# Pooling: a row's coefficients made among its elder neighbour's chunks and held, its outputs transposed into the places of u and v

## The chip, the cores and the metric

The kernel runs on one core of a Trainium2 chip. The metric is the device time of one execution in microseconds (us), the median of three runs. Five engines share the core's on-chip memory: TensorE (PE in the profile, its weight loads PEld), VectorE (DVE), ScalarE (ACT), GpSimd (POOL) and SyncE (SP), which only issues transfers here. Each engine works through its own instructions in a fixed order, and waits at the head of that order for what an instruction needs.

## The reference

The input x is 16 rows of 512 x 512 floats (512 positions S, 512 features D). Two residual blocks follow each other, both per row:

```python
h = gelu(x @ fc1_w.T + fc1_b)                                  # 512 -> 2048
x = x + concat([h @ fc2_w.T + fc2_b,                           # 384 features
                h @ experts_w[idx].T + experts_b[idx]], -1)    # 128 features, the row's expert
scores = tanh(x @ W1 + b1) @ v                                 # one number per position
mask = (l <= j, l >= j, l != j)[ptype]                         # one of three kinds per row
p = softmax(where(mask, scores, -1e30), -1)
x = x + (p @ x) / cnt                                          # the pooling
```

The three masks make the pooling of a row a running sum from the left, one from the right, or the sum of everything but the position itself. So no 512 x 512 product is needed: a recurrence along the positions, with coefficients made of the 512 scores, gives the result.

## The kernel before

The rows go in eight pairs i = 0..7. For a pair, fc1 is one Strassen-like product of 7 outer products, `Outer` n = 0..6, each of 7 inner products in two halves. An outer product is a loop of 14 steps k (a step is 4 matmul records in the trace, about 0.865 us of TensorE); the second half runs 5 steps behind the first, so that the last steps of an `Outer` run within the next one. After each inner product a short addition or copy brings its result from PSUM (the matmuls' output memory) to the on-chip memory: VectorE at L604, L618, L629, L641 and L645, ScalarE at L602, L620 and L625, with gelu at L591, GpSimd at L632. PSUM has few banks (three "bx", three "by", one "bd"), so TensorE's later product waits for these. GpSimd also makes the differences of the next outer product's input (`outer_sum` L292, `inner_sums` L314). Then come fc2 of row 0 and fc2 of row 1 (products "1", "2", "5", "7", "6", "3", "4"), whose result is x1T, the row after the first block, transposed.

The pooling of a finished row is a `Pooling` object, worked off a little at a time beside later matmuls. `project` and `score` (L851, L860) make the scores on TensorE; ScalarE copies them to two short rows `srow` (L863, L864), and two DMAs bring them into s2, a 32 x 16 layout (L867). What follows is a Python generator, `run_all`:

- `weights` (L969 to L1071): 43 small VectorE instructions, most on 32 x 16 numbers, and one exp on ScalarE (L1018), turn scores to coefficients. MAX8 and FIND_INDEX8 (L982, L984) find the largest score, and `at_maximum` lets GpSimd read x at its position (L934). The coefficients go to a DRAM tile `co_d` by two DMAs and come back as `cb`, spread over all 128 partitions (L1086 then mirrors a part).
- `apply`, for each of four chunks dc of 128 features: `weigh` (u = x1T times a coefficient, L1114, L1117), `recur` (the scan along the positions, L1125, and U, L1126), `offset` (ScalarE makes v, L1151, L1152), `finish` (f and the addition into x1T, L1133, L1143). u and v have one buffer each of 128 x 1024, f two of 128 x 512.
- four `flip`s: VectorE transposes x1T's chunk back by 32 x 32 blocks into a tile `yo` (L1193), and four DMAs store it to the output. The tag "yo" has two buffers, which `srow` and the last row's `spread` use as well.

The generator yields an estimate of its VectorE time after each bit, or a negative number for a pause. The order is written out by hand: `slot(SPARE[n], 0.86)` after each step of fc1, `slot(SPARE_2[name], 3.4)` within fc2. `Pooling.slot` takes bits from the generator until the slot's budget is used up. The function `slot` serves only the oldest unfinished row in the list `pools`; the next row's steps begin when it is done. `drain(1)` after fc1 and `drain()` after row 0 run what is left at once. SP's queue issues the weight loads (a ring of ten tiles of 256 KB), and co_d, cb and the output stores; ScalarE's queue issues s2 and the residual's input.

The even row of a pair has its coefficients in fc2 of row 1, its `apply` at the end of row 1 and in n = 0..2 of the next pair's fc1, with the flips in n = 4 and 5. The odd row is projected at k = 6 and scored at k = 11 of n = 0 of that fc1; its coefficients come at n = 5, n = 6 and in row 0, its `apply` and flips at the end of row 0. The last two rows, 14 and 15, have their own arrangement at the end.

Of the kernel before, what the change touches and what calls it, by code (L numbers as in the profile page):

```python
# [9 lines left out]
F32 = mybir.dt.float32  # L10
# [7 lines left out]
def tile_cond_experts_then_prompt_pool(  # L18
# [17 lines left out]
    P = 128  # L36
    B, _, ND, S = xT.shape
# [21 lines left out]
    p1 = ctx.enter_context(tc.tile_pool(name="p1", bufs=1))  # L59
# [104 lines left out]
    class Ring:  # L164
        def __init__(self):
            self.plan, self.tiles = [], {}
            for i in range(B // 2):
                b = 2 * i
                for o in OUTER:
                    self.plan += [("f1", i, o, p) for p in (INNER if i else INNER_0)]  # L170
                for r in range(2):
                    self.plan += [("up", b + r, "a11", h) for h in range(4)]
                    if not r:
                        self.plan += [("ex", b, "a11", h) for h in range(2)]
                    self.plan += [("up", b + r, "a12", h) for h in range(4)]
                    self.plan += [("ex", b + r, "a12", h) for h in range(2)]
                    self.plan += [("lo", b + r, n, h) for n in LOWER for h in range(2)]
                    if not r:
                        self.plan += [("ex", b + 1, "a11", h) for h in range(2)]
            self.at = 0  # L180
            self.taken, self.free = [], set()
# [135 lines left out]
    def bank(tag, name):  # L317
        return ps_m.tile([P, 2, HC], F32, tag=tag, name=name, bufs={"bx": 3, "by": 3, "bd": 1}[tag])
# [510 lines left out]


    TAGS = ("bx", "bx", "bx", "bd")
    co_d = dram.tile([2, ROW], F32, name="co_d")

    class Pooling:


        def __init__(self, b, x1T):
            self.b, self.x1T = b, x1T
            self.last = b == B - 1
            self.queue = nc.gpsimd if b == B - 2 else nc.sync  # L840
            self.turn = nc.vector.snap(nc.vector.value_load(ptype[b : b + 1].unsqueeze(0), min_val=0, max_val=2) % 2)
            self.steps = self.run_all()
            self.pause = self.credit = 0
            self.sent = False
            self.done = False

# [22 lines left out]
        def last_scores(self):  # L869

            self.y = [bank(t, f"y_{k}").rearrange("p m s -> p (m s)") for k, t in enumerate(TAGS)]
            for dc in range(ND):
# [22 lines left out]
            return copy  # L895


        def slot(self, budget, passed):
            self.pause -= passed
            if self.pause > 0:  # L900
                return
            self.credit = min(self.credit + budget, max(budget, 3.5))
            while self.credit > 0 and not self.done:
                t = next(self.steps, None)
                if t is None:
                    self.done = True
                elif t < 0:
                    if budget < 1e6:
                        self.pause = -1.7 * t
                        if passed < 1:  # L910
                            self.credit = 0
                        return
                else:
                    self.credit -= t
# [7 lines left out]
        def at_maximum(self, i8):  # L922
            b, eng = self.b, nc.scalar if self.last else nc.gpsimd
            jm = eng.value_load(i8[0:1, 0:1], min_val=0, max_val=S - 1)
            if self.last:
                jm = eng.snap((jm % SG) * SL + jm // SG)
                self.j_fix = jm
            self.x_max = self.x1T[:, :, ds(jm, 1)].rearrange("p k o -> p (k o)")
            self.xm = p1.tile([P, ND], F32, tag="xm", name=f"xm_{b}")
            self.eng = eng  # L930
            if self.last:
                eng.activation(self.xm, self.x_max, AF.Copy, scale=is2[:, b : b + 1])
            else:
                eng.tensor_tensor(self.xm, self.x_max, is2[:, b : b + 1].to_broadcast([P, ND]), ALU.mult)  # L934

        def run_all(self):
            yield from self.weights()
            yield from self.apply()
            if self.b < B - 3:
                yield -2  # L940
                for dc in range(ND):
                    store = self.flip(dc)
                    yield 0.7
                    yield -1
                    store()
                    yield -1

        def weights(self):
            V, b = nc.vector, self.b
            W = 32  # L950

            def small(name, shape, dt=F32):
                return p1.tile(shape, dt, tag=f"c_{name}", name=f"{name}_{b}")
# [99 lines left out]
            t = small("t", [SG, SL])  # L1053
# [23 lines left out]
            row = co_d[b % 2]  # L1077
            self.queue.dma_start(row[: 3 * S].rearrange("(k p c) -> p k c", k=3, c=SL), co)
            self.queue.dma_start(row[3 * S : 3 * S + 3].unsqueeze(0), sc[0:1, :3])
            yield -2  # L1080
            cb = self.cb = p1.tile([P, ROW + 2 * S], F32, tag="cb", name=f"cb_{b}")
            self.sent = True
            self.queue.dma_start(cb[:, 2 * S : ROW + 2 * S - 1], row[: ROW - 1].partition_broadcast(P))
# [105 lines left out]

        def flip(self, dc, yo=None):  # L1190
            if yo is None:
                yo = p1.tile([P, S], F32, tag="yo", name=f"yo_{self.b}_{dc}", bufs=2)
            nc.vector.transpose(yo, self.x1T[:, dc, :])  # L1193
            to = out[self.b].rearrange("(c j) (k a i) -> k a j c i", j=32, a=4, i=32)

            def store():
                for a in range(4):
                    nc.sync.dma_start(to[dc, a], yo[ts(a, 32), :].rearrange("j (c i) -> j c i", i=32))

            return store  # L1200
# [7 lines left out]
    pools = []  # L1208

    def slot(budget, passed):  # L1210
        while pools and pools[0].done:
            pools.pop(0)
        if pools:
            pools[0].slot(budget, passed)

    def drain(left=0):
        while len(pools) > left:
            slot(1e9, 1e9)


# [10 lines left out]
    for i in range(B // 2):  # L1231
# [9 lines left out]
        for n in range(7):  # L1241
# [8 lines left out]
            for k in range(14):  # L1250
# [29 lines left out]
                if n or k >= 8:  # L1280
                    slot(SPARE[n], 0.86)
# [4 lines left out]
        if i == 0:  # L1286
# [3 lines left out]
            flush_stores()  # L1290
            xr_next[:] = [residual(0, 0, 0), residual(0, 1, 1)]
        drain(1)
        for row in range(2):
            b = b0 + row
# [3 lines left out]
            def at(name):  # L1298
# [40 lines left out]
                if b + 1 == B:  # L1339
                    if name == "1b":  # L1340
                        pool.rush()
                    elif name == "2":
                        before_last.flip_all("xT")
                    elif name == "end":
                        pool.flip_all("tx")
                    elif name in LAST_2:
                        slot(LAST_2[name], 1.7)
                elif row and name == "4a":

                    slot(SPARE_2["3m"] * 0.4, 5.1)  # L1350
                elif name in SPARE_2 and not (row and name in ("3m", "3", "4m")):
                    slot(SPARE_2[name] * (0.4 if row and name in ("7m", "6m") else 1), 3.4)
                if b + 1 == B and name == "3":
                    drain()

            psc, x1T = fc2(b, hT[:, row], experts, at)
            if row == 0:
                experts = nxt["ex"]
                drain()
            elif more:  # L1360
                x_next, xi_next, xi_after = nxt["x"], nxt["xi"], nxt["xi_2"]
# [47 lines left out]
```

## Time and profile before

| | before |
|---|---|
| median of 3 runs | 1599.04 us (1598.66 to 1599.4) |
| the profiled execution | 1603.34 us, of which the span on the core is 1601.6 us |
| mean granted TensorE clock | 0.992 of full speed |
| one pair's fc1 (pairs 1 to 7) | 90.5 to 92.4 us |
| one row's fc2 | 101.1 us |
| first pair's fc1, tail after the last fc2 | 99.9 us, about 25 us |
| input read, output written | 253.55 MB, 29.45 MB |

The profiled execution is one execution with a profiler beside it. Its busy times are per engine; since the engines work beside each other they don't add up to the span. A line of the timeline gives start, duration, engine, source line, operation, output and inputs by name, and in square brackets how long the engine stood idle before it and what ended that. A line of the waits gives who waited for whom, the time in total, how often, and the longest one.

### The profile page before, as it was taken

To read this page: it belongs to the slowest core of one execution; us is meant where nothing else is said; L and a number is where in the kernel's file an instruction comes from. 1 tells how busy PE (TensorE), PEld (TensorE's weight loads), DVE (VectorE), ACT (ScalarE), POOL (GpSimd) and SP (SyncE) were. 2 spreads that over 40 slices of the span, in tenths; PEclk is the share of its full clock that TensorE was granted. 3 is DMA by queue.
4 is the path that set the end of the run, shared out by engine and by line. 5 is a ranking of instruction groups with operands and counts; after the bars stand their busy time and mean duration, and the time that the engine had idled before them with its cause. 6 is when DMAs were issued, how large, how long until landed. Compare 5 with 4: busy or idle time off the path is not lost. (4 is left out here: it accounts for less than half of the span.)

```text
span 1601.6 us, 21969 instructions
## 1 busy us (share of the span) xinstructions
PE 1565.5 (98%) x6986; PEld 1317.3 (82%) x6986; DVE 1160.8 (72%) x2108; ACT 620.9 (39%) x1244; POOL 391.7 (24%) x426
## 2 busy tenths in 40 slices
PE   7999999999999999999999999999999999999996
PEld 6788878888788888888888887888878888788884
DVE  7874657957677676777678785786757867668776
ACT  2350145422453324633246223462244521454333
POOL 5641015200350004500054000630015200260020
PEclk9999999999999999999999999999999999999997
DMA  7666646658466574666656675566745658466442
GB/s 269 218 216 211 207 128 165 191 156 262 117 176 194 148 240 133 175 204 164 201 147 180 198 209 154 156 190 182 217 149 160 193 160 259 118 169 184 154 99 53
DMA packets 340094, 284.54 MB, mean 178 GB/s; under 512 B 145292, under 2 KB 264140, under 8 KB 339980
## 3 DMA queue, kind: packets, MB, share of 16 engines
q1 hardware_dynamic: 313580, 244.23, 53.4%
q0 software_dynamic: 5760, 19.97, 3.8%
q10 hardware_dynamic: 20640, 18.94, 3.7%
q8 instruction: 56, 0.92, 0.2%
q14 instruction: 58, 0.48, 0.1%
HBM read 253.55 MB, written 29.45 MB: 177 GB/s over the span
## 5 line engine op out<-in xcount | busy, mean ns | idle before, releaser
L591 ACT ACTIVATE hT<-hT,fc1b_sb 128x256 f32<-128x256 f32 x416 | 179.7, 498 | 65.0 <-DVE hT L645 50.7
L632 POOL TENSOR_TENSOR q<-p,hT 128x512 f32<-128x512 f32 x80 | 106.0, 1325 | 368.9 <-ACT p L625 365.1
L574 PE MATMUL bx<-xi,w_f_s_s 128*128 128x256 f32 x512 | 129.7, 385 | 5.0 <-DVE ba L618 2.6
L724 PE MATMUL ba<-hT,w_up_a 128*128 128x256 f32 x512 | 116.7, 381 | 0.0
L574 PEld LDWEIGHTS bx<-xi,w_f_s_s 128*128 128x128 f32 x512 | 96.2, 191 | 24.5 <-DVE ba L618 8.0
L724 PEld LDWEIGHTS ba<-hT,w_up_a 128*128 128x128 f32 x512 | 96.5, 190 | 23.1 <-issue 10.7
L724 PE MATMUL bb<-hT,w_up_a 128*128 128x256 f32 x512 | 113.1, 379 | 0.0
L724 PE MATMUL bd<-hT,e 128*128 128x256 f32 x496 | 112.1, 379 | 0.0
L724 PEld LDWEIGHTS bb<-hT,w_up_a 128*128 128x128 f32 x512 | 97.3, 190 | 13.2
L724 PEld LDWEIGHTS bd<-hT,e 128*128 128x128 f32 x496 | 94.2, 190 | 12.8
L464 POOL DMA_INDIRECT e<-in_expT,rows x32 | 33.0, 1031 | 278.9 <-PE bd L724 273.9
L604 DVE TENSOR_TENSOR hT<-bx,hT 128x512 f32<-128x512 f32 x112 | 75.4, 685 | 32.6 <-PE bx L574 32.3
L1086 ACT COPY cb<-cb 128x1024 f32<-128x1024 f32 x15 | 15.7, 1045 | 210.5 <-DMA cb<-co_d 181.7
L574 PE MATMUL bx<-xi,w_f_a_s 128*128 128x256 f32 x384 | 95.4, 381 | 1.2 <-ACT ba L620 0.5
L625 ACT COPY p<-bd 128x512 f32<-128x512 f32 x112 | 65.4, 584 | 74.8 <-PE bd L574 72.9
L629 DVE TENSOR_TENSOR by<-bx,p 128x512 f32<-128x512 f32 x112 | 77.6, 692 | 21.7 <-PE bx L574 21.2
L1151 ACT ACTIVATE v<-f,U,cb 128x512 f32<-128x512 f32 x60 | 48.9, 815 | 107.6 <-DVE U L1126 102.2
L1125 DVE TENSOR_TENSOR_SCAN f<-cb,u 128x512 f32<-128x512 f32 x60 | 79.6, 1327 | 12.9 <-ACT u L1117 12.3
L1193 DVE STREAM_TRANSPOSE yo<-x1T 128x512 f32<-128x512 f32 x60 | 41.2, 701 | 63.4 <-DMA out_y<-yo 61.0
L680 ACT ACTIVATE xr<-xr,fc2b_sb 128x256 f32<-128x256 f32 x96 | 44.9, 500 | 106.2 <-DVE p1x L743 50.9
L1133 DVE TENSOR_TENSOR f<-v,cb 128x512 f32 x60 | 46.1, 769 | 53.9 <-ACT v L1152 53.9
L574 PEld LDWEIGHTS bx<-xi,w_f_a_s 128*128 128x128 f32 x384 | 72.1, 190 | 13.3 <-ACT ba L620 2.1
(292 smaller groups left out, 3495.7 us busy)
## 6 DMA issues: line engine op xcount, KB each, us to landing
w_up_a<-in_fc2T SPq DMA_DIRECT2D x128, 256.0 KB
w_lo_s<-w2s_s SPq DMA_DIRECT2D x128, 256.0 KB
w_f_s_s<-w1s_s_s SPq DMA_DIRECT2D x112, 256.0 KB
w_f_a_s<-w1s_a_s SPq DMA_DIRECT2D x84, 256.0 KB
w_f_s_a<-w1s_s_a SPq DMA_DIRECT2D x84, 256.0 KB
w_f_a_a<-in_fc1T SPq DMA_DIRECT2D x69, 256.0 KB
w_ex_a<-in_fc2T SPq DMA_DIRECT2D x64, 256.0 KB
xr<-in_xT ACTq DMA_DIRECT2D x64, 256.0 KB
```

The source lines that it names most:

```text
L574: nc.tensor.matmul(to.rearrange("p (b s) -> p b s", b=2) if len(mv.shape) == 3 else to, w[:, ts(2 * mh + m, P)], mv, start=(not add and m ...
L591: nc.scalar.activation(to[:, m], src[:, m], AF.Gelu, bias=fc1b_sb[:, hc + m : hc + m + 1])
L604: eng.tensor_tensor(to, src, self.place(prev, r, c, mh)[1], ALU.add)
L625: nc.scalar.copy(u["p5"], bd)
L629: add(u["y"], u["x"], u["p5"], ALU.add)
L632: nc.gpsimd.tensor_tensor(self.both(u["q"]), self.both(u["p5"]), self.place(self.to[0][1], 1, 1, mh)[1], ALU.add)
L680: nc.scalar.activation(t[:, m, :], t[:, m, :], AF.Identity, bias=bias)
L724: nc.tensor.matmul(bank[:, m, :], w(m, k), mv[:, k, :], start=(not add and m == 0 and k == 0), stop=(k == depth - 1), skip_group_check=True,)
L1125: V.tensor_tensor_scan(f[dc], c0, turned(u[dc]), 0.0, ALU.mult, ALU.add)
L1133: V.tensor_tensor(f[dc], turned(v[dc]), beta, ALU.mult)
L1151: nc.scalar.activation(v[dc][:, :S], f[dc], AF.Identity, bias=U[:, dc : dc + 1], scale=fac)
L1193: nc.vector.transpose(yo, self.x1T[:, dc, :])
```

## The change

While the oldest row of the list has its coefficients sent (its `sent` is set), the next row's generator now gets the slots first. It runs until it has stored its coefficients to `co_d` and yields `HOLD`; it is then held, and the oldest row continues. The held row goes on once it is itself the oldest, and only then are its `cb` and the rest allocated. So in fc1 the odd row's coefficients come directly after its scores, in n = 1 and 2, among the even row's chunks; the even row's `apply` stretches to n = 5, and its flips come in n = 6. The tile `xm` gets two buffers, as two rows now need it at a time.

The flips no longer use the tag "yo". Two flips share one tile of 128 x 2 x 512, the first two in the place of u, the other two in the place of v. One of the two pauses per flip is gone. `drain` counts the rows that are not done, rather than the list's length.

```diff
+    HOLD = -99
...
+            self.held = False
...
         def slot(self, budget, passed):
             self.pause -= passed
             if self.pause > 0:
                 return
+            self.held = False
...
                 elif t < 0:
+                    self.held = t == HOLD
                     if budget < 1e6:
-                        self.pause = -1.7 * t
+                        self.pause = -1.7 * (-2 if self.held else t)
...
-            self.xm = p1.tile([P, ND], F32, tag="xm", name=f"xm_{b}")
+            self.xm = p1.tile([P, ND], F32, tag="xm", name=f"xm_{b}", bufs=2)
...
                     store()
-                    yield -1
...
             self.queue.dma_start(row[3 * S : 3 * S + 3].unsqueeze(0), sc[0:1, :3])
-            yield -2
+            yield HOLD
             cb = self.cb = p1.tile([P, ROW + 2 * S], F32, tag="cb", name=f"cb_{b}")
             self.sent = True
...
         def flip(self, dc, yo=None):
             if yo is None:
-                yo = p1.tile([P, S], F32, tag="yo", name=f"yo_{self.b}_{dc}", bufs=2)
+                if dc % 2 == 0:
+                    self.yo = p1.tile([P, 2, S], F32, tag=("u", "v")[dc // 2], name=f"yo_{self.b}_{dc}")
+                yo = self.yo[:, dc % 2, :]
...
     def slot(budget, passed):
         while pools and pools[0].done:
             pools.pop(0)
+
+        if len(pools) > 1 and budget < 1e6 and pools[0].sent:
+            pools[1].pause -= passed
+            if pools[1].pause <= 0 and not pools[1].held:
+                pools[0].pause -= passed
+                pools[1].slot(budget, 0)
+                return
         if pools:
             pools[0].slot(budget, passed)
 
     def drain(left=0):
-        while len(pools) > left:
+        while sum(not p.done for p in pools) > left:
             slot(1e9, 1e9)
```

## The prediction, made before the changed kernel had run

> **What bounds the kernel now.** I read the shares of the span first, then TensorE's own waits, VectorE's waits, and last the timeline around each TensorE gap. Line numbers are those of the kernel before.
>
> ```profile
> PE 1565.5 (98%) x6986; PEld 1317.3 (82%) x6986; DVE 1160.8 (72%) x2108; ACT 620.9 (39%) x1244; POOL 391.7 (24%) x426
> ```
>
> TensorE is the bound, and the work it is given stays the same: only its gaps can move. Counting, stage by stage, how far its matmul records (0.216 us each when back to back) stretch, I find 17.0 us lost in the seven fc1 stages of pairs 1 to 7 together, about 0.2 us in each fc2, 3.8 us in the last fc2, 15.6 us in the first fc1; a tail of 25 us follows. The change touches neither the first fc1 nor the tail, so at most some 20 us can be won. Who ends those gaps:
>
> ```profile
> PE bx L574 <- DVE hT L641: 3.3, 8, 2.0
> PE bx L574 <- DVE hT L645: 3.3, 6, 0.9
> PE bx L574 <- DVE ba L618: 2.8, 5, 1.3
> ```
>
> Columns: us, times, longest. In all three TensorE waits for an fc1 addition on VectorE, queued behind a pooling instruction. VectorE's own longest waits are two pooling waits:
>
> ```profile
> DVE yo L1193 <- DMA out_y<-yo: 61.0, 33, 3.4
> DVE f L1133 <- ACT v L1152: 53.9, 38, 3.4
> ```
>
> A VectorE wait costs only where an fc1 addition behind it comes too late. There are two such spots per fc1. Spot A, at the start of n=1, here in pair 2:
>
> ```profile
> 419.09 0.69 DVE L1133 TENSOR_TENSOR f<-v,cb 128x512 f32 x1 [3.32 <-ACT v L1152]
> 419.70 0.68 DVE L641 TENSOR_TENSOR hT<-bx,p 128x512 f32<-128x512 f32 x1
> 420.44 1.13 PE L574 MATMUL bx<-xi,w_f_a_a 128*128 128x256 f32 x4 [0.17 <-DVE hT L641]
> 421.64 0.73 PEld L574 LDWEIGHTS bx<-xi,w_f_s_s 128*128 128x128 f32 x4 [0.48 <-DVE ba L618]
> ```
>
> Finish waits 3.32 us for ScalarE, L641 stands behind it, TensorE twice comes to a stop (0.34 and 0.24 us, and about 0.1 us to restart each time). Spot B, n=4 and 5, in pair 3: a flip waits 3.41 us for an earlier store, L645 behind it, TensorE 0.92 us.
>
> ```profile
> 657.44 0.71 DVE L1193 STREAM_TRANSPOSE yo<-x1T 128x512 f32<-128x512 f32 x1 [3.41 <-DMA out_y<-yo]
> 658.07 0.65 DVE L645 TENSOR_TENSOR hT<-bx,q 128x512 f32<-128x512 f32 x1
> ```
>
> B costs 0.68, 0.48, 1.58, 0.53, 0.34, 1.50 and 1.93 us in pairs 1 to 7: 7.0 us.
>
> **The change part by part.** The built program's instruction order tells where things go.
>
> *Flips out of the yo ring.* The elder row's flips come in n=6, four waits on stores in n=4 and 5 vanish: −7.0 us. In their place the longer apply of the elder row (its scans of n=5) lies ahead of L618 and L645; its scan of 1.2 to 2.05 us is longer than the slack of some rows there. I take +0.3 us per pair, +2.0 us (0 to 0.6 each). The younger row's flips stay at the end of row 0, with no fresh wait; fc2 has only 0.2 us to give. The flips' stores are on SP, behind nothing new; the later u_0 and v_0 wait for stores that are then many us old. Row 14's L775 is no longer behind a finish: TensorE's wait at pa L851 (0.4 us, 0.7 with what follows) goes, −0.7. Pair 3's late cb (0.69 us at n=2) loosens: −0.4 (0 to −0.8). SP's two co_d stores come four n earlier, ahead of weight loads that a ring of ten keeps far ahead of use: 0. The exp table loads that move out from among gelus are on ScalarE, 39% busy: 0.
>
> *Spot A with new work.* The younger row's coefficients now begin here: L969 to L982 come ahead of L641, L984 ahead of L618. Finish moves to n=2, so its 3.3 us wait is no longer in front. But L970 needs s2, whose second half lands at 418.70 (2.95 us after the score's matmul ended at 415.75). The chain from L970 through MAX8 takes 1.44 us by row 14's uninterrupted pass (1519.14 to where the next instruction can start). L641 thus starts at 418.70+0.09+1.44=420.23 instead of 419.70: 0.53 us later. L984, 0.75 us, then precedes L618: TensorE's second start is about 422.25 instead of 421.64, +0.6 us. Seven pairs: +4.2 us. Bounds: −0.8 (both gaps gone) to +1.0 each. I take 0.6, since all its terms are rows. Offsets are the same in every pair to 0.02 us, so one working serves for all.
>
> *Coefficients under a busy GpSimd.* The 43 small instructions take 8.9 us in row 14's pass. Before, the odd row's ran in n=5, n=6 and row 0: between 480 and 493 GpSimd is busy 2.7 us of 13. Now they run in n=1 and n=2, where it is busy 9.6 us of 13 (427 to 440). The trace shows what that does: L969 and L970 under GpSimd's xi, and the same two alone in row 14.
>
> ```profile
> 477.42 0.78 DVE L969 TENSOR_SCALAR s<-s,not 32x16 f32<-32x16 f32 x1
> 478.24 0.65 DVE L970 SCALAR_TENSOR_TENSOR s<-s,is,s 32x16 f32<-32x16 f32 x1
> ```
> ```profile
> 477.45 0.73 POOL L314 TENSOR_TENSOR xi<-tx 128x256 f32<-128x256 f32 x1
> 478.13 0.73 POOL L314 TENSOR_TENSOR xi<-tx,xi 128x256 f32<-128x256 f32 x1
> ```
> ```profile
> 1518.49 0.22 DVE L969 TENSOR_SCALAR s<-s,not 32x16 f32<-32x16 f32 x1
> 1519.14 0.22 DVE L970 SCALAR_TENSOR_TENSOR s<-s,is,s 32x16 f32<-32x16 f32 x1 [0.43 <-DMA s<-srow]
> ```
>
> 0.78 and 0.65 against 0.22: each ends with the GpSimd instruction beside it. L987 likewise (1.13 to 1.15 against 0.16). The Trainium skill, "SBUF — State Buffer", section "Who interferes with whom", speaks against this change: VectorE and GpSimd share a pair of SBUF ports as an exclusive lock; a VectorE instruction with two SBUF inputs, or in a two-port mode (copy, tensor_scalar), stands still until the other's instruction ends. The trace agrees in part: L1126 and L1003, one element wide, and L1006, 17 wide, are not delayed. If I priced only the bare rows (0.2 us each), the move would cost about 0.2 us per pair. By the rule, n=2 goes thus:
>
> ```profile
> 433.89 1.28 POOL L632 TENSOR_TENSOR q<-p,hT 128x512 f32<-128x512 f32 x1 [3.31 <-ACT p L625]
> 435.12 2.95 POOL L292 TENSOR_TENSOR xT<-xT 128x512 f32<-128x512 f32 x2
> 438.04 1.18 POOL L314 TENSOR_TENSOR xi<-xT 128x256 f32<-128x256 f32 x1
> ```
> ```profile
> 434.97 0.70 DVE L629 TENSOR_TENSOR by<-bx,p 128x512 f32<-128x512 f32 x1 [0.24 <-PE bx L574]
> 435.58 1.37 DVE L1133 TENSOR_TENSOR f<-v,cb 128x512 f32 x1
> ```
>
> L1054, L1055 and L1056 now come between this L629 and L618, which starts at 436.87. They are a tensor_scalar and two instructions with two SBUF inputs, all 32x16. The first waits to 436.6 (end of the first L292), the second to 438.07, the third to the end of L314 at 439.22. L618 starts there, 2.35 us late, and ends at 439.9. TensorE's product that it frees is due at 438.15, with A's 0.6 at 438.75: 1.2 us of stop, 0.1 to restart, and 0.2 behind it at the next L629: 1.5 us per pair, +10.5. Bounds 0.2 (no lock) to 2.0 (GpSimd shifts with A too). I take 1.5, as L970 under xi is such an instruction under such another.
>
> **Sum.** −7.0 +2.0 −0.7 −0.4 +4.2 +10.5 = +8.6 us. The profiled execution's span of 1601.6 (1603.34 us with what lies around it) would become 1610.2; it stands 4.3 us above the median 1599.04, so on the median: 1607.6 us.
>
> **The rivals.** About 0.2% (3 us) is what a measurement here can tell from no change.
>
> *The flips' release wins (faster).* The wait L1193 for its store is a real TensorE gap, 7.0 us; the coefficients find gaps on a VectorE that is 72% busy, s2 comes in time. For it: L641's wait of 3.3 us on ScalarE goes. Against it: L969/L970 above. It decides below (7.0+1.1)/7=1.16 us of new cost per pair. With A and the lock at 0 and 0.2: −8.1+1.0+1.4=−5.7, 1593.3 us. Chance 0.21.
>
> *The lock spares n=2.* GpSimd's sums run a little earlier or later, or its L292 gives way: A's +4.2 remains, with 1.4 for the small instructions and 1.0 for B's successor: −8.1+6.6=−1.5, 1597.5 us, no difference. That the waits merely change place, one for one, ends here too. Chance 0.17.
>
> *The lock bites twice.* In n=1 as well, where L1003 to L1016 pass GpSimd's xi sums. Per pair 2.0 in n=2 and 0.4 in n=1: −8.1+2.0+4.2+16.8=+14.9, 1613.9 us. For it: GpSimd is busy 7 us of 12 there. It is within my slower case, whose chance is 0.62 in all.
>
> Range 1593 to 1613: between the first rival's forecast and the third's; it leaves out about half of the first and the worst of the third. The slower case alone: 1603 to 1614.
>
> **What would show it.** Right: L1193's wait for out_y near 0; L969/L970 ahead of L641 at spot A, TensorE waiting for L641 about 0.9 us in each pair; L1054 to L1056 at 0.7 to 1.5 us instead of 0.2 in n=2, a TensorE gap of about 1 us for L618 ahead of the third product after it; fc2 stages at 101.1 us as before. Wrong: L1054 to L1056 at 0.2 us, or L618 of n=2 without a gap (then the time falls to the second rival); a finish waiting longer among the gelus of n=4 and 5 would make it slower than I say.

## The result and the profile after

The changed kernel takes 1662.22 us (median of 4 runs, 1660.79 to 1664.22), the kernel before, beside it, 1599.22: a ratio of 1.0392, with a 95% interval of 1.0374 to 1.041. That is 63 us slower, where 8.6 us were forecast, and far outside the range.

One correction first: the 101.1 us that the table above gives for one row's fc2 are those of a pair's two rows together, and so are the fc2 times quoted below, also where an expectation says "fc2 of row 0".

The shares, and TensorE's waits:

```profile
PE 1584.6 (95%) x6986; PEld 1327.2 (80%) x6986; DVE 1176.2 (71%) x2108; ACT 602.2 (36%) x1230; POOL 388.5 (23%) x426
```
```profile
PE bc L724 <- DMA w_lo_s<-w2s_s: 32.0, 7, 4.8
...
PE bx L574 <- DVE ba L618: 5.7, 10, 0.7
PE bx L574 <- DVE hT L641: 5.7, 8, 1.0
...
PE bx L574 <- DVE hT L645: 0.8, 2, 0.6
```

The first line is new: seven times, once per pair, fc2 waits up to 4.8 us for its weights w_lo_s. L645, spot B, fell from 3.3 to 0.8 us as forecast; L641 and L618, spot A and n=2, rose. VectorE's wait of 61.0 us for the flips' stores (L1193) is gone from its list.

Counting lost matmul time by stage, as in the prediction, puts the span's 58.4 us more (1660.0 against 1601.6) in place:

| stage | lost before | lost after | difference |
|---|---|---|---|
| fc1 of pairs 1 to 7 | 17.0 | 22.9 (3.21 to 3.31 each) | +5.9 |
| fc2 of pairs 1 to 7 | 5.1 | 56.0 (7.7 to 8.5 each) | +50.9 |
| first fc1, start | 15.6 | 16.6 | +1.6 with the start |

So the interleaving's own cost is small, and nearly all of the loss lies in fc2, which I had ruled out. The place, in pair 2: SyncE's queue, ScalarE's queue, TensorE (columns: start, duration, engine).

```profile
506.15 5.01 SPq L1205 DMA_DIRECT2D out_y<-yo  x8
518.24 0.95 SPq L215 DMA_DIRECT2D w_ex_a<-in_fc2T  x2
519.27 1.88 SPq L213 DMA_DIRECT2D w_lo_s<-w2s_s  x4
```
```profile
515.44 0.39 ACTq L674 DMA_DIRECT2D xr<-in_xT  x1
```
```profile
523.63 6.50 PE L724 MATMUL bc<-t,w_lo_s 128*128 128x256 f32 x16 [4.47 <-DMA w_lo_s<-w2s_s]
```

The flips' last eight stores are issued by 511.2. Then SyncE stands still for 7 us ahead of the load of w_ex, with w_lo_s queued behind it. It goes on at 518.24, 2.8 us after ScalarE has issued a load of the residual. In the kernel before, the same loads followed each other without a stop, and came 9 to 10 us earlier with respect to fc2's start (493.3 there, 505.2 here):

```profile
496.60 1.55 SPq L215 DMA_DIRECT2D w_ex_a<-in_fc2T  x2
498.25 9.18 SPq L213 DMA_DIRECT2D w_lo_s<-w2s_s  x8
```

SyncE's waits name what it stood for, seven times, once per pair, a wait that the kernel before hasn't:

```profile
SPq L215 <- DMA xr<-in_xT: 47.7, 7, 7.6
```

But w_ex and xr have nothing to do with each other: different tiles, different inputs. What they share is a counter. The built program gives the transfers of SyncE and ScalarE together eight completion counters in rotation, and each transfer waits, before it is issued, until the previous one on its counter has landed; the trace's issues carry the same eight, and GpSimd's transfers others. (The Trainium skill, "DMA: Bandwidth & Descriptors", section "Why a DMA increments its semaphore by 16 and not by 1", tells why it must: with two transfers in flight on one counter, the count may be reached before the first has landed.) The rotation in both built programs at this place, counter after the colon:

```
before: w_ex:1 w_ex:2 w_lo_s1:3 w_lo_s1:4 w_lo_s3:5 w_lo_s3:6 xr:7 w_lo_s2:0 ... co_d:6 co_d:7
after:  out_y:3 xr:4 out_y:5 out_y:6 out_y:7 out_y:0 out_y:1 out_y:2 out_y:3 w_ex:4 w_ex:5 w_lo_s1:6 ...
```

The xr load itself waits, on ScalarE's queue, for its tile, which the addition p1x (L743, at 514.7 us) sets free. Before, the next on its counter was a store of co_d, much later. With the flips' stores moved to the end of fc1, xr falls among them, and the eighth transfer after it is the expert's weight load.

Last, what the stop costs beyond itself. A table by stretch (columns: from:to, length, busy us of PE, PEld, DVE, ACT and POOL with instructions, granted clock, DMA share, GB/s):

```profile
518.80:523.40 4.60, 0.37 (x2) 0.00 (x0) 2.04 (x3) 0.00 (x0) 0.00 (x0) 0.90 0.84 228
523.40:529.50 6.10, 5.87 (x14) 4.73 (x15) 2.24 (x2) 1.84 (x3) 0.00 (x0) 0.52 1.04 384
```

In the 6.1 us after the stop the granted clock is 0.52, and nearly all of the 14 matmul records there take 0.427 us in place of 0.216; then it is 1.00 again. So a stop of 4.6 us costs this pair 7.5 us (its fc2 takes 108.6 in place of 101.1). In the last pair the half clock lasts only half as long, 7 records.

### The profile page after: what moved, and what is told of

It is laid out like the page before. It is cut to its first block, busy times and chain, and to the rows that moved or that the text cites. A ratio compares the mean times of both kernels' runs of the same rounds, so it can differ in the third digit from the quotient of the medians.

```text
span 1660.0 us, 21950 instructions
## 1 busy us (share of the span) xinstructions
PE 1584.6 (95%) x6986; PEld 1327.2 (80%) x6986; DVE 1176.2 (71%) x2108; ACT 602.2 (36%) x1230; POOL 388.5 (23%) x426
## 5 line engine op out<-in xcount | busy, mean ns | idle before, releaser
L724 PE MATMUL bc<-t,w_lo_s 128*128 128x256 f32 x256 | 77.0, 468 | 32.0 <-DMA w_lo_s<-w2s_s 32.0
L724 PEld LDWEIGHTS bc<-t,w_lo_s 128*128 128x128 f32 x256 | 61.3, 243 | 46.2 <-DVE es L487 24.3
L1129 DVE TENSOR_TENSOR_SCAN f<-cb,u 128x512 f32<-128x512 f32 x60 | 73.6, 1226 | 13.2 <-ACT u L1121 12.5
```

The source lines that it names most:

```text
L724: nc.tensor.matmul(bank[:, m, :], w(m, k), mv[:, k, :], start=(not add and m == 0 and k == 0), stop=(k == depth - 1), skip_group_check=True,)
L1129: V.tensor_tensor_scan(f[dc], c0, turned(u[dc]), 0.0, ALU.mult, ALU.add)
```

## The experiments

The theory (A) is the shared counter. Its rival (B) is traffic: 16 stores in pieces of 128 bytes and cb's 770 KB stand ahead of the weights and fill the DMA engines, so that w_lo_s would be late whatever xr does. The changed kernel's own trace speaks against B: while SyncE stands still, the DMA engines are busy for 0.23 of the time (columns as in the last table).

```profile
511.20:518.20 7.00, 7.00 (x34) 6.15 (x34) 6.37 (x4) 0.00 (x0) 0.00 (x0) 1.00 0.23 56
```

**The residual given a tile of its own.** Row 0's second residual takes a tile of the tag yo, and needn't wait for p1x:

```diff
-        t = p1.tile([P, 2, HC], F32, tag="xr", name=f"xr_{b}_{r}{c}", bufs=2)
+        t = p1.tile([P, 2, HC], F32, tag="yo" if b % 2 == 0 and (r, c) == (0, 1) else "xr", name=f"xr_{b}_{r}{c}", bufs=2)
```

> The changed kernel, but for row 0 of each pair the second residual load takes its tile from the tag yo, so that it needn't wait for the first residual's tile to be free (the addition p1x). Theory A (shared counter): in the changed kernel SyncE's load of the expert weights w_ex, and all fc2 weight loads behind it, waited on a completion counter that the residual load holds until about 518 us of the span; here that load is issued some 7 us earlier, the fc2 of row 0 goes back from 108.6 to about 101.2 us, the time to about 1662-51=1611, or 1606 with fc1's share alone (+6 us over before). Theory B (traffic): the 16 output stores at the end of fc1 and the earlier cb load hold up the weight loads in the DMA engines; then nothing changes here, about 1660.

1617.33 us (1615.19 to 1618.79); ratio to before 1.0107 (1.0089 to 1.0124). The fc2 stages are at 102.2 to 102.9 us, with one stop of 0.8 to 1.8 us each. That is 45 us less than the changed kernel, which speaks for A, though 6 us more than the 1611 expected. What remains goes with a store that waits on a counter (SyncE's L1205 waits 4.4 us for an xr in pair 2). The clock keeps full speed after these stops.

**The even rows' stores on GpSimd.** Same stores, same time, another queue:

```diff
-                    nc.sync.dma_start(to[dc, a], yo[ts(a, 32), :].rearrange("j (c i) -> j c i", i=32))
+                    (nc.sync if self.b % 2 else nc.gpsimd).dma_start(to[dc, a], yo[ts(a, 32), :].rearrange("j (c i) -> j c i", i=32))
```

> The changed kernel, with the even rows' output stores issued by GpSimd instead of SyncE. Theory A: those stores no longer stand between the residual load and the weight loads in the order in which completion counters are given out, so the weight load doesn't share the residual's counter: about 1606 to 1611, fc2 of row 0 at about 101 us. Theory B: the stores move the same bytes in the same pieces at the same time; if the DMA engines are what is full, about 1655 to 1660.

1610.48 us (1609.7 to 1611.2), ratio 1.0066 (1.005 to 1.0082). All fc2 stages of pairs 1 to 6 are at 101.1 us; fc1 loses 3.20 to 3.29 us as in the changed kernel. The bytes are the same, so B falls as far as it speaks of the DMA engines.

**One load per pair on GpSimd's queue.** This leaves the stores, cb and SyncE's queue as they are, and xr as late as it was; only its counter is another:

```diff
-        nc.scalar.dma_start(t, xT[b][:, ts(r, 2), ts(c, HC)])
+        (nc.gpsimd if b % 2 == 0 and (r, c) == (0, 1) else nc.scalar).dma_start(t, xT[b][:, ts(r, 2), ts(c, HC)])
```

> The changed kernel, with one load per pair (row 0's second residual) issued by GpSimd instead of ScalarE: it still waits for the same addition p1x and lands at about the same time, but GpSimd's transfers count on counters of their own, so no weight load of SyncE shares one with it. The stores, cb and SyncE's queue stay. Theory A (shared counter): fc2 of row 0 from 108.6 us to 101.2 to 102.5 (as in the run with the residual apart), the time about 1608 to 1618. Theory B (the stores or the residual's own lateness): still 108 us, about 1660.

1608.91 us (1606.81 to 1611.14), ratio 1.0045 (1.003 to 1.006): 53 us less than the changed kernel, by the queue of one load per pair. (The kernel before took 1601.85 us beside this run, and 1599.22 beside the changed kernel; by the ratios it is 55 us.) SyncE's queue and the load, in this kernel's pair 2:

```profile
497.97 5.44 SPq L1205 DMA_DIRECT2D out_y<-yo  x8
503.51 0.99 SPq L215 DMA_DIRECT2D w_ex_a<-in_fc2T  x2
504.59 1.88 SPq L213 DMA_DIRECT2D w_lo_s<-w2s_s  x4
```
```profile
507.50 0.75 POOL L674 DMA_DIRECT2D xr<-in_xT  x1 [15.50 <-DVE p1x L743]
```

The residual is issued at 507.50, four microseconds after w_ex, which no longer waits for it, and eight stores stand directly ahead of w_ex. That decides for A.

**Each half of the change alone.** The flips' tiles alone (the two-tile lines of `flip` in the kernel before), and the interleaving alone (the changed kernel with the line below back).

```diff
-                if dc % 2 == 0:
-                    self.yo = p1.tile([P, 2, S], F32, tag=("u", "v")[dc // 2], name=f"yo_{self.b}_{dc}")
-                yo = self.yo[:, dc % 2, :]
+                yo = p1.tile([P, S], F32, tag="yo", name=f"yo_{self.b}_{dc}", bufs=2)
```

> The kernel before, with only the flips' tiles moved to the places of u and v (no interleaving of two rows). Forecast's step: the flips' waits for older stores in n=4 and 5 cost 7.0 us and vanish: 1592 (1590 to 1594); fc2 at 101.1 us as before. Rival: a wait takes their place (the next row's u and v wait for the stores): 1597 to 1601, no change.

1608.55 us (1607.14 to 1608.84), ratio 1.0051 (1.0037 to 1.0065): both expectations missed. fc1 does what the forecast's step said: it loses 1.30 to 1.33 us in every pair, 9.2 in place of 17.0. But fc2 takes 102.8 to 104.9 us. Its waits show the same trap at another place, row 1, where 16 stores of the odd row come together (one of the seven waits, of 7.0 us, the kernel before has too):

```profile
SPq L1200 <- DMA xr<-in_xT: 23.2, 7, 7.0
```

So the tiles alone gain 7.8 us in fc1, and fc2's losses rise from 5.1 to 17.2 us. The 104.9 us are pair 1's, where the clock fell after the stop.

> The changed kernel with the flips' tiles back in the ring yo (the interleaving alone). Theory A: in the built order of this kernel the residual load shares its counter with a weight load that is needed much later, so fc2 stays near 101 us; fc1 carries spot A and the small instructions of n=2, and the flips wait for stores again: 1606 to 1613. Theory B: the coefficients are still ahead and the stores still at fc1's end: about 1655 to 1660.

1610.08 us (1608.42 to 1613.57), ratio 1.006 (1.0044 to 1.0077), as expected, and fc2 of pairs 1 to 6 is at 101.1 us, though the coefficients are as early as in the changed kernel. SyncE waits for xr here too, once per pair:

```profile
SPq L213 <- DMA xr<-in_xT: 38.1, 7, 6.1
```

But the load that shares xr's counter is the fourth w_lo_s of the same row. In pair 2 w_ex and three w_lo_s were issued ahead of it, between 504.33 and 506.84; only then SyncE stood still, until 512.37, and TensorE did not stop. So a wait on a shared counter costs something only when what stands behind it is needed soon. fc1 loses 3.21 to 3.74 us, and 6.29 in pair 4, where the clock fell (see the end).

**Flips' tiles, with stores on GpSimd.** For the odd rows, then for all:

```diff
-                    nc.sync.dma_start(to[dc, a], yo[ts(a, 32), :].rearrange("j (c i) -> j c i", i=32))
+                    (nc.gpsimd if self.b % 2 else nc.sync).dma_start(to[dc, a], yo[ts(a, 32), :].rearrange("j (c i) -> j c i", i=32))
```

> The kernel with the flips' tiles alone moved (1608.5 us), and the odd rows' output stores issued by GpSimd. In the former, fc1 lost 1.30 us per pair (before 2.4 on the mean), but fc2 of row 1 lost 2.1 us where SyncE, amid 16 stores, waited for counters shared with loads of ScalarE. Theory A: with the stores off SyncE that loss goes: fc2 at 101.1 us, 1591 (1589 to 1595), faster than before. Theory B: the late weight loads come from the stores' traffic: still about 1607.

1595.68 us (1593.87 to 1599.42), ratio 0.9965 (0.9953 to 0.9977). fc1 loses 1.30 us, fc2 of pairs 1 to 6 takes 101.1. That is just above the 1595 at the end of the range given, and B falls here too. This version beats both kernels, if only by 0.35%.

> As the former, with the even rows' stores on GpSimd too: they lie in n=4 and 5 of fc1, where VectorE and GpSimd share work. Theory A: the same as the former within 0.2%, 1589 to 1595, as no counter is shared there. If GpSimd's issuing (16 stores per row) delays its sums q and xi: up to 1600, with TensorE gaps in n=4 to 6.

1604.52 us (1600.16 to 1607.19), ratio 1.0017 (1.0006 to 1.0028), so the expectation of theory A was missed; the second one, a cost on GpSimd, holds in kind, though the time is above its 1600. fc2 is at 101.1 us, but fc1 loses 2.3 to 2.9 us. GpSimd, then VectorE, in pair 2:

```profile
479.71 1.93 POOL L1200 DMA_DIRECT2D out_y<-yo  x3
481.64 1.28 POOL L632 TENSOR_TENSOR q<-p,hT 128x512 f32<-128x512 f32 x1
```
```profile
482.95 0.69 DVE L645 TENSOR_TENSOR hT<-bx,q 128x512 f32<-128x512 f32 x1 [2.31 <-POOL q L632]
```

Issuing a store takes GpSimd 0.65 us. Three of them ahead of q make L645 late, and TensorE stops 0.6 and 0.4 us. In fc2 (the run before this one), or in n=6 where the sums are done (the run with the even rows' stores on GpSimd), the same issues cost nothing that shows.

**The small instructions under GpSimd's sums.** In the changed kernel, VectorE and GpSimd in n=2 of pair 2:

```profile
446.56 0.83 DVE L1058 TENSOR_SCALAR t<-co,q 32x16 f32<-32x16 f32 x1
447.43 1.19 DVE L1059 SCALAR_TENSOR_TENSOR z<-z,not,t 32x16 f32<-32x16 f32 x1
448.65 0.65 DVE L1060 TENSOR_TENSOR z<-z,cnt 32x16 f32<-32x16 f32 x1
```
```profile
446.10 2.50 POOL L292 TENSOR_TENSOR xT<-xT 128x512 f32<-128x512 f32 x2
448.55 0.73 POOL L314 TENSOR_TENSOR xi<-xT 128x256 f32<-128x256 f32 x1
```

The three (the prediction's L1054 to L1056) end at 447.4, 448.6 and 449.3, as the GpSimd instructions beside them end. To test the cause, the two L292 are issued four steps earlier (on the kernel with even rows' stores on GpSimd, 1610.48 us):

```diff
-                    if k == 4:
+                    if k == (0 if n == 2 else 4):
                         x.outer_sum(n + 1, nc.gpsimd)
```

> The changed kernel with the even rows' stores on GpSimd (1610.5 us), and GpSimd's two sums L292 for n=3 issued at step 0 of n=2 instead of step 4, so that they don't lie beside the three small instructions ahead of L618 (0.83, 1.19 and 0.65 us in the changed kernel). Forecast's step (each small instruction stands still until GpSimd's beside it ends): two of them fall to 0.3 us, the gap of 0.94 us in n=2 goes to 0 to 0.3 and fc1 from 92.0 to about 91.2 us: 1605. Rival (they are long for their own reason, or DVE is just full): no change, 1610.

1601.98 us (1599.78 to 1605.02), ratio 1.0002 (0.9991 to 1.0012): 8.5 us less, or 10 by the ratios, more than the 5 I expected.

```profile
439.94 0.28 DVE L1058 TENSOR_SCALAR t<-co,q 32x16 f32<-32x16 f32 x1
440.25 0.62 DVE L1059 SCALAR_TENSOR_TENSOR z<-z,not,t 32x16 f32<-32x16 f32 x1
440.90 0.16 DVE L1060 TENSOR_TENSOR z<-z,cnt 32x16 f32<-32x16 f32 x1
```

2.67 us of small instructions became 1.06, and fc1 loses 1.85 us in place of 3.26: all of n=2's share. The instructions are the same; only what runs beside them differs. (In the kernel before, the second of them took 0.22 us in all 16 rows.)

**Spot A.** Two runs hold back what stands ahead of L641: on the last kernel neither row gets a slot for five steps after the score; on the fastest kernel the elder row is paused.

```diff
+            if pools[1].fresh and pools[1].pause > 0:
+                pools[0].pause -= passed
+                return
+            pools[1].fresh = False
             if pools[1].pause <= 0 and not pools[1].held:
...
                         pools.append(pool)
+                        pool.pause, pool.fresh = 4.0, True
```

> The former (even rows' stores on GpSimd, L292 of n=2 early), and after the score neither row gets a slot for five steps, so that the younger row's first coefficient instructions no longer stand ahead of L641 and L618 at the start of n=1. Forecast's step for spot A (waiting for s2 and the search for the maximum cost TensorE 1.35 us per pair there): the two gaps of 0.84 and 0.30 us with their restarts go, fc1 loses about 0.5 us instead of 1.86, 7 x 1.3 = 9 us: 1593 beside 1602, if the elder row's later apply and flips cost nothing at the end of fc1. Rival (the gap is the addition's own lateness on TensorE's side): 1602.

1612.83 us (1611.15 to 1614.72), ratio 1.0069 (1.0055 to 1.0082): missed. The two gaps at the start of n=1 are gone, but fc1 loses 3.3 us in place of 1.85: what follows is later, and a new wait comes at the end of n=3, 1.1 us per pair for GpSimd's sum xi:

```profile
PE bx L574 <- POOL xi L314: 7.7, 7, 1.2
```

```diff
                         pool.score()
+                        if pools:
+                            pools[0].pause = 4.0
                         pools.append(pool)
```

> The fastest so far (flips' tiles moved, odd rows' stores on GpSimd, no interleaving: 1595.7), with the elder row held for five steps after the score, so that its finish, which waits for ScalarE, comes behind L641 and L618 (spot A as it was in the kernel before: 0.34 and 0.24 us with 0.1 each to restart). If that is what spot A is: fc1 loses 0.5 us instead of 1.30, 7 x 0.8 = 5.6 us: 1590. If the elder's later steps only move the gap: 1596.

1621.58 us (1619.2 to 1623.87), ratio 1.0131 (1.0113 to 1.0148): in fc1 as expected, 0.52 us lost in place of 1.30, so spot A is what I took it for. But the time is 20 us longer than the kernel before's, as the pooling left over is later: L775 now stands behind pooling instructions at the end of row 0, and row 1's projection waits for it:

```profile
PE pa L851 <- DVE x1T L775: 20.6, 7, 3.0
```

fc2 loses 3.9 to 5.6 us per pair for it.

## Why the prediction was wrong

Its fc1 half was right in its mechanisms, if 3.4 us too high; its statement about fc2 was wrong.

- *Spot B.* Forecast −7.0 us, gone as said; the flips' tiles alone take fc1 from 17.0 to 9.2 us, −7.8. The +2.0 us that I put in its place (a scan ahead of L618 in n=5) did not come: the changed fc1's losses are A, n=2 and what was there anyway.
- *Spot A.* Forecast +0.6 us per pair from s2's arrival and the search for the maximum. Measured: gaps of 0.84 and 0.30 us with their restarts, 1.35 against 0.78, +0.57.
- *n=2.* Forecast 1.5 us per pair by the port rule, with L618 2.35 us late. Measured 0.94 us for L618 and 0.46 for what follows, 1.40. The early-sums run shows the cause. The prediction counted the 17 wide L1006 as not delayed; in the changed kernel it took 0.57 to 0.61 us in seven rows, in place of 0.27, and ended with a GpSimd sum each time.
- *fc1 in all.* Forecast +9.3 us (−7.0 +2.0 −0.4 +4.2 +10.5), measured +5.9. The 2.0 us that did not come make most of the difference. TensorE's wait for row 14's L775, 0.4 us, is gone as said.
- *The failed step.* "The flips' stores are on SP, behind nothing new", "ahead of weight loads that a ring of ten keeps far ahead of use: 0", and "fc2 has only 0.2 us to give". I put the whole move of SyncE's transfers at nothing. I asked what stands ahead of the stores, and whether something waits for their tiles. I did not ask what stands behind them: SyncE's loads of fc2's weights, which in the kernel before were issued only some 9 us ahead of their use (498.25, for the third product, which starts about 507). Nor did I follow what each issue waits for: in the changed kernel w_ex stood 7 us for an xr that shared its counter, and w_lo_s behind it came too late. "fc2 has 0.2 us to give" is a bound on a gain, and I read it as a bound on a loss. The cost was 50.9 us: seven stops of 4.6 us on the mean, 32.0 in all, and 18.9 for the rest, nearly all of it the half clock after them.
- *What the forecast is worth without it.* With one load moved to another queue the changed kernel takes 1608.91 us, 7.1 more than the kernel before beside it; 8.6 were forecast. That they are so close is in part luck: fc1 had 3.4 us too much in the forecast, and the two profiled spans differ by 5.7.
- *The rivals.* The third, the lock at more places, had no part in the 50.9 us. None named a transfer queue; the slower case's end of 1613.9 us was too near, as it only varied terms already in the sum.

## What to carry to other kernels

When transfers move on an in-order queue, list what is issued after them until the next load that TensorE needs, and for each the counter it is given and the transfer that held it before: with eight counters in rotation, a load can be held by the transfer eight places earlier, on another engine's queue, that waits for something of its own. The built program's order and waits show this before any run; whether it costs anything depends on how soon what stands behind the held load is needed. A stage that loses nothing bounds what a change can win there, not what it can lose.

## What the runs showed of the hardware

The half clock. In these traces the granted clock changes only on a raster of 3.41 us, and what tells the falls apart from the rest is how long TensorE stood still within one interval of it. I counted 0.216 us as busy for each matmul record at full clock (twice that for the scores' wider ones), in all twelve traces from 20 to 1570 us. After every interval with 2.1 us or more of standstill the clock was at half in the next one; with 2.05 us or less it never fell. So the length of a stop alone does not tell:

- a stop of 3.1 us, which an interval's end can cut in two, cost the clock in two pairs of seven (the last run);
- one of 2.1 us cost it in pair 1 of the flips' tiles alone, and five of 1.7 to 2.0 us there did not;
- in the interleaving alone, L641's wait of 1.56 us with the short gaps around it cost it in pair 4's fc1 (columns as above):

```profile
813.76:817.17 3.41, 3.41 (x9) 2.70 (x8) 2.08 (x6) 0.19 (x1) 2.65 (x4) 0.50 0.21 77
```

Full speed came back after the first interval with at most 0.5 us of standstill; with 0.76 us or more the clock stayed at half. That is why the half clock of the changed kernel lasted two intervals in six pairs: the rest of the stop, 0.85 to 1.9 us, lay in the first. The Trainium skill, "TensorE: Matmul & The Clock Gate", Part 1, gives a free-running window of about 3.4 us, an idle one for the fall and a busy one for the return. The length agrees; but a window that stood still for 2.1 us of its 3.41 was enough for the fall here.

A small instruction that stands still: the same instruction on 32x16 numbers took VectorE 1.19 us beside GpSimd and 0.22 us alone, and moving GpSimd's work by four steps was worth 1.4 us in each of seven pairs.
